# Order of the score products in an attention kernel: long blocks of all four heads ahead of the short ones

## The chip, the cores and the metric

The kernel runs on one core of a Trainium2 chip. The metric is the device time of one execution in microseconds; the median of several executions is given. The core has five engines that run side by side, each taking its own instructions in order and waiting on semaphores for the others: TensorE (PE, matrix products into PSUM), ScalarE (ACT), VectorE (DVE), GpSimd (POOL) and SyncE (SP, which issues transfers). A matmul has a stationary operand, whose load is an instruction of its own (PEld in the profile), and a moving operand whose columns stream past it. The array can be addressed in row groups of 32 partitions, so products with a 32-long contraction can stand side by side in it.

## What is computed

For 32 images of 256 channels and 1024 positions: a group normalisation, a masked self-attention with 8 heads of 32 channels, and a residual addition. All in float32.

```python
q  = einsum('oc,bcs->bos', q_w, xf) + q_b          # xf: normalised x, (32, 256, 1024)
kv = einsum('oc,bcs->bos', kv_w, xf) + kv_b
mask = tril(ones((S, S)), -1)                      # a query sees only earlier positions
scores = einsum('bhqd,bhkd->bhqk', q, k) / sqrt(dk)
scores = where(mask == 0, -10000.0, scores)
attn = softmax(scores, axis=-1)
attn = where(mask == 0, 0.0, attn)
out = einsum('bhqk,bhkd->bhqd', attn, v)
return x + out
```

## The kernel before

**Tiling.** The scores are kept transposed, keys on the partitions and queries in the columns. A group `g` is four heads (four times 32 channels fill the 128 partitions of a `q` and a `k` tile), so head `j` of a group lies in the partitions 32j to 32j+31, which is row group `j` of the array. The 1024 queries are two halves (`hf`) of 512. For one key block of 128 (`k`) and one half, `piece` says which queries are needed, since a key block is seen only by later queries. For most key blocks that is one stretch of 512 or 256 queries. Where the key block is the second one on the diagonal of its half (`d == 1`), 384 queries remain, and the free 128 columns are filled with the last key block of that half (`k + 2`), which needs 128 queries. Such a piece has two entries in `blocks`; the others have one.

**Visits.** The work on an image is a fixed list of 12 visits, 6 for each group. A visit takes one `full` piece (512 columns for each of four heads) and one `half` piece (256 columns for each):

```python
visits += [
    (f[0][0], f[0][2]), (f[0][1], h[1, 0]), (f[1][0], h[1, 1]),
    (f[1][3], h[2, 0]), (f[1][4], h[2, 1]), (f[1][5], f[1][6]),
]
```

`f[0][1]` and `f[1][5]` are the pieces with two blocks, so 4 of the 12 visits of an image have them: 128 of the 384 visits in all.

**Scores of a visit.** `scores` takes three PSUM tiles `sT` of two banks each. `pairs[0]` holds the full piece of heads 0 and 1, `pairs[1]` that of heads 2 and 3 (one bank per head), and `pairs[2]`, called `short`, holds the half piece of all four, two heads in a bank. TensorE is given: the half piece of heads 2 and 3; the full piece of heads 0, 1, 2, 3; then, behind a wait on the semaphore `bank_free` [...], the half piece of heads 0 and 1. Each float32 matmul of the program is two matmul instructions in the trace, called the first and the second pass here, each with its own weight load. A visit with one block in its full piece is therefore 16 matmul instructions, one with two blocks 24.

**What follows.** ScalarE takes the exponential of the three tiles (L331 twice, L329 once), GpSimd zeroes the masked queries on the diagonal (L292), VectorE adds the exponentials up for the softmax's sum (L358), and one visit later TensorE multiplies them with `v` into `acc` (`values`, L353). Between scores and values of a step, TensorE runs one unit of the projections of the next image (`project_qk` and `project_v`, both through `product`, L169). The main loop (L612 on) writes this order out by hand for all engines but SyncE; no scheduler moves an instruction.

**Lines of the prediction.** L272 to L282 is `scores_of`, whose loop over `blocks` sets the order within a head; L309 to L311 and L321 are its calls; L277 is the matmul itself.

Of the kernel before, what the change touches and what calls it, by code (L numbers as in the profile page):

```python
# [17 lines left out]
P = 128  # L18
HD = 32
CPG = 8  # L20
HALF = 512
# [10 lines left out]
def tile_norm_attention_residual(  # L32
# [19 lines left out]
    nc = tc.nc  # L52
# [56 lines left out]
    def unshifted():  # L109
        live = {}  # L110
# [158 lines left out]
                blocks = [(k, slice(0, HALF), slice(0, HALF))]  # L269
            return g, hf, k, part, tuple(blocks)  # L270

        def scores_of(pc, pair, j):  # L272

            b, (g, hf, k, part, blocks) = pc
            rows = slice(HD * j, HD * (j + 1))
            for kb, cols, of in blocks:
                ins = nc.tensor.matmul(  # L277
                    pair[:, cols], lhsT=live["k", b, g][rows, kb * P : (kb + 1) * P],
                    rhs=live["q", b, g][rows, hf * HALF + of.start : hf * HALF + of.stop],
                    start=True, stop=True, skip_group_check=True,  # L280
                )
            return ins  # L282

        def mask(pc, e):


            g, hf, k, part, blocks = pc
            if k < hf * BPH:
                return
            n = len(blocks)  # L290
            diagonal = e[:, :, : n * P].rearrange("p j (n q) -> p j n q", q=P)
            nc.gpsimd.affine_select(  # L292
                out=diagonal, in_=diagonal, pattern=[[0, 4], [0, n], [1, P]],
                compare_op=ALU.is_gt, fill=0.0, base=0, channel_multiplier=-1,
            )
            if k == 0:
                nc.gpsimd.memset(e[0:1, :, 0:1], 1.0)

        def scores(b, full, half, between=()):

            tag = "e0" if full[2] == 0 else "e"
            name = f"{b}_{full[0]}_{full[1]}_{full[2]}"
            e = epool.tile([P, 4, HALF], F32, tag=tag, bufs=4 if tag == "e0" else 3, name=f"{tag}_{name}")
            eh = epool.tile([P, 4, HALFBANK], F32, tag="eh", bufs=4, name=f"eh_{name}")
            pairs = [ps_s.tile([P, 2, HALF], F32, tag="sT", name=f"sT_{name}_{a}") for a in range(3)]
            short = pairs[2].rearrange("p bank (n q) -> p bank n q", n=2)
            first = [scores_of((b, half), short[:, j % 2, 1, :], j) for j in (2, 3)]  # L309
            for j in range(4):  # L310
                scores_of((b, full), pairs[j // 2][:, j % 2, :], j)  # L311

            for ins in first:
                ins.then_inc(bank_free, 1)
                tc.no_tile_sem_insts.add(ins.ins.name)
            live["free"] = live.get("free", 0) + len(first)
            wait = nc.tensor.wait_ge(bank_free, live["free"])
            for ins in first:
                tc.declare_no_dep(wait.ins, ins.ins, reason="the semaphore orders them")
            for j in range(2):  # L320
                lo = scores_of((b, half), short[:, j, 0, :], j)  # L321
                for ins in first:
                    tc.declare_no_dep(lo.ins, ins.ins, reason="the semaphore orders them")
            for a in (0, 2, 1) if between else (0, 1, 2):
                if a == 1:
                    for f in between:
                        f()
                if a == 2:
                    exp = nc.scalar.activation(eh.rearrange("p (n bank) q -> p bank n q", n=2), short, AF.Exp)  # L329
                else:  # L330
                    nc.scalar.activation(e[:, 2 * a : 2 * a + 2, :], pairs[a], AF.Exp)  # L331

            for ins in first:
                tc.add_to_no_dep_group(f"first_{name}", ins.ins)
                tc.add_to_no_dep_group("first", ins.ins)
            tc.declare_no_dep(exp.ins, group=f"first_{name}", reason="through the last two products")
            tc.declare_fence(exp.ins, group=f"first_{name}")
            mask(full, e)
            mask(half, eh)
            live["e", b, full], live["e", b, half] = e, eh  # L340
# [210 lines left out]
        with tc.manual_schedule(engines={ENG.PE, ENG.Activation, ENG.DVE, ENG.Pool}):  # L551
# [60 lines left out]
            for i in range(B * N + 1):  # L612
                if i < B * N:

                    between = at.pop(i, ()) if i % N == 6 else ()
                    scores(i // N, *visits[i % N], between)
                for f in at.pop(i, ()):
                    f()
                if i:
                    for pc in products[(i - 1) % N]:  # L620
                        values((i - 1) // N, pc, i < B * N - 1)
                for f in after.pop(i, ()):
                    f()
# [159 lines left out]
```

## Time and profile before

| | |
|---|---|
| Median of 3 executions | 1878.86 us (1873.87 to 1880.27) |
| Span of the profiled execution | 1874.0 us |
| TensorE busy | 1850.8 us, 99% |
| VectorE busy | 1573.4 us, 84% |
| ScalarE busy | 1413.7 us, 75% |
| GpSimd busy | 765.5 us, 41% |
| Score matmuls (L277) | 7168 instructions |
| Mean granted TensorE clock | 0.997 |

A row of busy time is the union of the engine's instructions, and matmuls of different row groups overlap, so 99% says that TensorE nearly always had something in flight, not that its array was full. The profile models the end of a matmul; its start is recorded. A matmul's duration in the tables runs from its recorded start, so it contains the time for which it stood behind its own weight load. The start of the next block of work is the reading to trust for how long a block took.

### The profile page before, as it was taken

To read this page: it belongs to the slowest core of one execution; us is meant where nothing else is said; L and a number is where in the kernel's file an instruction comes from. 1 tells how busy PE (TensorE), PEld (TensorE's weight loads), DVE (VectorE), ACT (ScalarE), POOL (GpSimd) and SP (SyncE) were. 2 spreads that over 40 slices of the span, in tenths; PEclk is the share of its full clock that TensorE was granted. 3 is DMA by queue.
4 is the path that set the end of the run, shared out by engine and by line. 5 is a ranking of instruction groups with operands and counts; after the bars stand their busy time and mean duration, and the time that the engine had idled before them with its cause. 6 is when DMAs were issued, how large, how long until landed. Compare 5 with 4: busy or idle time off the path is not lost.

```text
span 1874.0 us, 54145 instructions
## 1 busy us (share of the span) xinstructions
PE 1850.8 (99%) x23410; PEld 950.6 (51%) x23410; DVE 1573.4 (84%) x1604; ACT 1413.7 (75%) x1775; POOL 765.5 (41%) x741
## 2 busy tenths in 40 slices
PE   8999999999999999999999999999999999999997
PEld 4555555555554555555555545455555555455543
DVE  3778988888988889888889888898888888888878
ACT  5777777777777777777777777777777777777775
POOL 1443443434434434434344344343343443443413
PEclk9999999999999999999999999999999999999998
DMA  3446665666666666665666656766556666666412
GB/s 119 69 79 144 138 145 118 117 137 138 140 123 127 125 140 139 145 121 111 137 138 142 145 105 123 140 138 148 117 114 140 138 143 116 133 123 140 95 50 81
DMA packets 77516, 233.41 MB, mean 125 GB/s; under 512 B 19808, under 2 KB 20832, under 8 KB 61912
## 3 DMA queue, kind: packets, MB, share of 16 engines
q0 software_dynamic: 15360, 94.39, 34.4%
q1 hardware_dynamic: 60280, 134.72, 24.7%
q8 instruction: 185, 3.03, 0.7%
q10 hardware_dynamic: 1632, 0.79, 0.1%
q14 instruction: 59, 0.48, 0.1%
HBM read 68.41 MB, written 35.62 MB: 56 GB/s over the span
## 4 chain that ended last, share of the span: by engine, by line
PE 97%; DVE 1%; DMA 0%; ACT 0%; issue 0%; ACTq 0%; DVEq 0%
PE sT L277 31%; PE acc L353 26%; PE pp L169 25%; PE ppv L169 13%; PE pd L390 2%; DVE e L358 1%; DMA wn<-in_L_conv_kv_w_dram 0%; DVE rb L464 0%; DVE rb L463 0%; DVE rb L478 0%; ACT e L331 0%; PE pv L169 0%; PE busy L155 0%; ACT k L231 0%; PE pm L169 0%
## 5 line engine op out<-in xcount | busy, mean ns | idle before, releaser
L331 ACT ACTIVATE e<-sT 128x1024 f32<-128x1024 f32 x768 | 748.3, 1022 | 365.4 <-PE sT L277 283.2
L358 DVE TENSOR_TENSOR e<-e,eh 128x1024 f32<-128x1024 f32 x382 | 534.5, 1413 | 247.2 <-PE acc L353 215.1
L292 POOL TENSOR_SCALAR_AFFINE_SELECT e<-e 128x512 f32<-128x512 f32 (+1 forms) x256 | 359.4, 1404 | 678.5 <-ACT e L331 657.9
L358 DVE TENSOR_TENSOR e<-e,e 128x1536 f32<-128x1536 f32 x381 | 618.0, 1622 | 16.9 <-POOL e L292 2.6
L277 PE MATMUL sT<-q,k 32*128 32x256 f32 (+3 forms) x7168 | 617.6, 460 | 0.8 <-ACT k L231 0.8
L277 PEld LDWEIGHTS sT<-q,k 32*128 32x128 f32 x7168 | 463.4, 184 | 163.7 <-ACT q L231 50.6
L169 PE MATMUL pp<-xn,wT 128*32 128x512 f32 x4096 | 492.2, 598 | 0.0
L353 PE MATMUL acc<-e,v 128*32 128x512 f32 (+2 forms) x4096 | 401.1, 486 | 0.0
L329 ACT ACTIVATE eh<-sT 128x1024 f32<-128x1024 f32 x384 | 395.6, 1030 | 0.0
L371 POOL DMA_DIRECT2D e<-e x240 | 199.5, 892 | 388.0 <-PE sT L277 159.5
L169 PE MATMUL ppv<-wT,xn 128*32 128x256 f32 x4096 | 247.3, 382 | 0.0
L353 PEld LDWEIGHTS acc<-e,v 128*32 128x32 f32 x4096 | 132.9, 110 | 223.6 <-issue 201.1
L353 PE MATMUL acc<-eh,v 128*32 128x256 f32 x3072 | 224.4, 379 | 0.0
L169 PEld LDWEIGHTS pp<-xn,wT 128*32 128x32 f32 x4096 | 107.0, 109 | 218.2 <-issue 199.3
L353 PEld LDWEIGHTS acc<-eh,v 128*32 128x32 f32 x3072 | 98.5, 110 | 164.2 <-issue 152.6
L169 PEld LDWEIGHTS ppv<-wT,xn 128*32 128x32 f32 x4096 | 120.2, 109 | 102.0 <-issue 32.1
L292 POOL TENSOR_SCALAR_AFFINE_SELECT eh<-eh 128x512 f32<-128x512 f32 x128 | 160.6, 1255 | 0.1
L464 DVE SCALAR_TENSOR_TENSOR rb<-rb,v_bias_col,x 128x512 f32<-128x512 f32 (+1 forms) x127 | 114.1, 898 | 4.5
L463 DVE TENSOR_TENSOR rb<-num,rb 128x512 f32<-128x512 f32 (+1 forms) x127 | 90.4, 711 | 11.6 <-DMA rb<-inverses 11.3
L231 ACT ACTIVATE k<-pp,qk_bias 128x512 f32<-128x512 f32 x128 | 89.4, 698 | 13.5 <-PE pp L169 12.4
L214 DVE TENSOR_SCALAR xn<-x,mean,rstd 128x512 f32<-128x512 f32 x128 | 96.7, 796 | 2.0 <-POOL rstd L207 2.0
L231 ACT ACTIVATE q<-pp,qk_bias 128x512 f32<-128x512 f32 x128 | 89.9, 702 | 4.0 <-PE pp L169 4.0
(69 smaller groups left out, 515.2 us busy)
## 6 DMA issues: line engine op xcount, KB each, us to landing
e<-e POOLq DMA_DIRECT2D x120, 512.0 KB, 8.0
x<-in_x_dram SPq DMA_DIRECT2D x64, 512.0 KB
out_dram<-rb SPq DMA_DIRECT2D x127, 256.0 KB
rb<-inverses SPq DMA_DIRECT2D x126, 256.0 KB
e<-e POOLq DMA_DIRECT2D x120, 256.0 KB, 5.0
folded<-e SPq DMA_DIRECT2D x120, 256.0 KB
rows<-sums SPq DMA_DIRECT2D x31, 32.0 KB
inverses<-inv SPq DMA_DIRECT2D x31, 32.0 KB
```

Source lines behind the costliest of these rows:

```text
L169: nc.tensor.matmul(out[part], lhsT=lhsT[:, part], rhs=rhs, start=start, stop=stop, skip_group_check=True)
L214: nc.vector.tensor_scalar(live["xn", b][:, g, cols], live["x", b][:, g, cols], mean[:, g : g + 1], rstd[:, g : g + 1], ALU.subtract, ALU.mult,
L231: nc.scalar.activation(live[key][:, cols], pp, AF.Identity, bias=qk_bias[:, n, g : g + 1], scale=(SCALE, 1.0)[n],)
L277: ins = nc.tensor.matmul(pair[:, cols], lhsT=live["k", b, g][rows, kb * P : (kb + 1) * P], rhs=live["q", b, g][rows, hf * HALF + of.start ...
L292: nc.gpsimd.affine_select(out=diagonal, in_=diagonal, pattern=[[0, 4], [0, n], [1, P]], compare_op=ALU.is_gt, fill=0.0, base=0, channel_mu ...
L329: exp = nc.scalar.activation(eh.rearrange("p (n bank) q -> p bank n q", n=2), short, AF.Exp)
L331: nc.scalar.activation(e[:, 2 * a : 2 * a + 2, :], pairs[a], AF.Exp)
L353: nc.tensor.matmul(acc[HD * j : HD * (j + 1), of], lhsT=live["v", b][:, kb, h * HD : (h + 1) * HD], rhs=e[:, j, cols], start=first, stop=l ...
L358: nc.vector.tensor_add(total[:, :, of], total[:, :, of], e[:, :, cols])
L371: nc.gpsimd.dma_start(out=total[:rows], in_=total[rows : 2 * rows], accum_op=ALU.add)
L463: nc.vector.tensor_mul(rb, num[:, within], rb)
L464: nc.vector.scalar_tensor_tensor(rb, rb, v_bias_col[:, g : g + 1], xt[:, g, cols], ALU.add, ALU.add)
```

## The change

In a visit whose full piece has two blocks, the order on TensorE was head by head: 384 queries of head 0, 128 of head 0, 384 of head 1, 128 of head 1, and so on. After the change it is block by block: 384 queries of heads 0 to 3, then 128 queries of heads 0 to 3. The half piece stays where it was, two heads ahead and two behind. Its purpose is that neighbouring instructions belong to different row groups, as they do already in the visits with one block. Nothing is added or removed: the same 24 matmuls of such a visit run with the same operands into the same PSUM columns, and the other 256 visits have the order that they had. The order of ScalarE, VectorE, GpSimd and SyncE is the same.

```diff
-        def scores_of(pc, pair, j):
+        def scores_of(pc, pair, j, n=0):
 
             b, (g, hf, k, part, blocks) = pc
             rows = slice(HD * j, HD * (j + 1))
-            for kb, cols, of in blocks:
-                ins = nc.tensor.matmul(
-                    pair[:, cols], lhsT=live["k", b, g][rows, kb * P : (kb + 1) * P],
-                    rhs=live["q", b, g][rows, hf * HALF + of.start : hf * HALF + of.stop],
-                    start=True, stop=True, skip_group_check=True,
-                )
-            return ins
+            kb, cols, of = blocks[n]
+            return nc.tensor.matmul(
+                pair[:, cols], lhsT=live["k", b, g][rows, kb * P : (kb + 1) * P],
+                rhs=live["q", b, g][rows, hf * HALF + of.start : hf * HALF + of.stop],
+                start=True, stop=True, skip_group_check=True,
+            )
...
             first = [scores_of((b, half), short[:, j % 2, 1, :], j) for j in (2, 3)]
-            for j in range(4):
-                scores_of((b, full), pairs[j // 2][:, j % 2, :], j)
+
+
+            for n in range(len(full[4])):
+                for j in range(4):
+                    scores_of((b, full), pairs[j // 2][:, j % 2, :], j, n)
```

## The prediction

> **What bounds the kernel now.** I read the page's first part, then TensorE's own waits, then the middle of the run in one window (100 to 1700 us: PE busy 1598.24 of 1600.00 us), then two visits in the timeline, then the score matmuls kept apart by shape.
>
> ```profile
> span 1874.0 us, 54145 instructions
> PE 1850.8 (99%) x23410; PEld 950.6 (51%) x23410; DVE 1573.4 (84%) x1604; ACT 1413.7 (75%) x1775; POOL 765.5 (41%) x741
> ```
>
> TensorE is the bound. Its waits (engine, line, what it waited for: us in total, times, longest) confirm that nobody holds it up:
>
> ```profile
> PE wt L148 <- DMA wn<-in_L_conv_q_w_dram: 5.1, 1, 5.1
> PE pd L390 <- DVE e L358: 2.1, 1, 2.1
> ...
> PE sT L277 <- ACT k L231: 0.8, 1, 0.8
> ```
>
> The scores waited once, for 0.8 us, in the whole run. So what a visit costs is decided inside TensorE, and time taken out of it comes off the end unless it turns into a wait. Now a visit with one block, a visit with two, and what follows each (start us, length us, ...):
>
> ```profile
> 899.98 1.57 PE L277 MATMUL sT<-q,k 32*128 32x256 f32 x16
> 901.48 1.93 PE L169 MATMUL ppv<-wT,xn 128*32 128x256 f32 x32
> ...
> 904.73 1.67 PE L277 MATMUL sT<-q,k 32*128 32x256 f32 x24
> 906.33 1.92 PE L169 MATMUL pp<-xn,wT 128*32 128x512 f32 x16
> ```
>
> Read start to next start: 901.48 - 899.98 = 1.50 us with 16 matmuls, 906.33 - 904.73 = 1.60 us with 24. Both stream the same 768 columns through each row group. Going through the trace's starts of all 384 visits, the one-block visits take 1.502 to 1.503 us, and the two-block visits 1.600 us but for the last two (2.23 us). The difference, 0.098 us in each of 128 visits, is all that an order can win: **12.5 us**.
>
> Where do the 0.098 us sit? The shapes tell (count | busy us, mean ns of one | idle):
>
> ```profile
> L277 PE MATMUL sT<-q,k 32*128 32x256 f32 x3072 | 499.4, 400 | 0.8 <-ACT k L231 0.8
> L277 PE MATMUL sT<-q,k 32*128 32x512 f32 x2048 | 395.6, 613 | 0.0
> L277 PE MATMUL sT<-q,k 32*128 32x384 f32 x1024 | 184.6, 520 | 0.0
> L277 PE MATMUL sT<-q,k 32*128 32x128 f32 x1024 | 112.6, 269 | 0.0
> ```
>
> In the two visits of the timeline, a matmul whose weights were loaded ahead is recorded with 374 ns (256 columns), 481 (384) and 587 (512); one that starts together with its load has 478, 585 and 692, so 104 to 105 ns more. The means count the late loads. For 512: (2 x 692 + 6 x 587) / 8 = 613, two of eight per visit, the unavoidable first ones of heads 0 and 1. For 384: 520 = (3 x 585 + 5 x 481) / 8: **three** of eight. One load per two-block visit is late, always.
>
> [...] in the visit at 904.73 head 1's 384-query matmul starts at 904.752, while head 0's 128-query one, ahead of it in the program, starts at 905.488. [...]
>
> **The change, step by step.** Starts in the visit at 904.73 (us past 904), first and second pass each:
> - head 3: half piece .732, 1.052; 384 queries 1.268, 1.694; 128 queries 2.016, 2.125; then 107 ns of streaming to 2.232, and the next product starts at 2.325.
> - head 2: .725, 1.045; 1.261, 1.584; 1.906, 2.015.
> - head 1: 384 queries .752, 1.179; 128 queries 1.501, 1.610; half piece 1.722, 1.940; end 1.940 + .213 = 2.153.
>
> Between the passes of the 384 block lie 323 ns in head 2 but 426 in head 3. Head 3's load for it is recorded at 1.265, just after head 2's block began (1.261); head 2's own load was at 1.047. In the one-block visit the same two loads lie 7 ns apart (900.299, 900.306). The reason I read from the program order: [...] 17 loads and matmuls ahead of head 3's load have not started, since the 128-query blocks of heads 0, 1 and 2 stand in between; in the one-block visit it is 5. Head 1's half-piece load still came in time (1.613) with 11 unstarted ahead. [...]
>
> After the change 5 stand ahead of head 3's load, and at most about 10 ahead of any other (the half-piece load of head 1), so none is late. Then:
> - head 3: 1.268 + .323 = 1.591, + .322 = 1.913, + .109 = 2.022, end 2.129. It gains 103 ns and is no longer last.
> - head 1 becomes last. Its first issue moves up by some 7 ns (heads follow each other by 7 ns in the one-block visit, 13 here), so its end is 2.146.
> - plus the same 92 ns to the next product: 2.238 in place of 2.325.
>
> Saving 0.087 us x 128 visits = **11.1 us**; 1878.86 - 11.1 = **1867.8 us**. Of the 103 ns in head 3, 16 are lost because head 1's chain takes over. Rearranging the remaining 23 matmuls costs nothing: same shapes, same weights, each in its own row group.
>
> **What could hand it back.** The wait for `pairs[1]` to be empty now stands ahead of the 128-query blocks of heads 0 and 1. It is over long before:
>
> ```profile
> 905.99 1.94 ACT L331 ACTIVATE e<-sT 128x1024 f32<-128x1024 f32 x2 [0.86 <-DVE e L358]
> 907.81 1.03 ACT L329 ACTIVATE eh<-sT 128x1024 f32<-128x1024 f32 x1
> ```
>
> The last exponential of this visit ends at 908.84, the next scores start at 909.47: 0.63 us of slack, of which the change eats 0.09. The first exponential waits for head 1's second 128-query pass (1.610 before, 1.603 after), so it keeps its place in the visit. If completions were signalled in program order it would wait for head 3's 384 block too, some 0.2 us later, still inside the slack. VectorE, at 84%, would have 1573.4 / 1863 = 84.5%. [...]
>
> **Rivals.**
> 1. The whole difference goes: two-block visits become as short as the others, 12.5 us, 1866.4 us. For: the columns are equal. Against: head 1's chain has two more passes to start, and measures 1.188 us from first to last start against 1.178 in the one-block visit.
> 2. No gain: the late load is not a matter of place in the queue [...], or the saving comes back as waits. 1878.9 us. Against: 128-query passes average 269 ns, with their own loads in time; the slack is 0.63 us.
> 3. Slower: the late load moves to a head that has no reserve. One late load in head 1 puts its end at 2.253, the next product at 2.345, 0.020 us later than now: +2.6 us, 1881.5 us. Two in a row would give 0.127 us: +16 us, 1895 us. For: block-by-block order packs heads 0 and 1 tighter. Against: their loads have fewer unstarted instructions ahead than before.
>
> **Chances.** My forecast 0.72, rival 1 0.10, rival 2 0.13, rival 3 0.05. The executions before spread from 1873.87 to 1880.27, so I take 3 us either way around forecast and rival 1 and let the range reach partway to rival 2: 1862.5 to 1874. Faster by over 0.3% (5.6 us) 0.82, within 0.13, slower 0.05.
>
> **What would show it.** Right: two-block visits of 1.51 us start to next start; mean of the 384-query matmuls 507 ns (2 x 585 + 6 x 481, by 8) in place of 520, those of 512, 256 and 128 unchanged; head 3's first 384 load some 7 ns after head 2's; no new TensorE wait over 1 us. Wrong: two-block visits still at 1.60 us, or shorter visits with the span unchanged and a TensorE wait on ACT or POOL in their place.

## The result and the profile after

The time did not move. The changed kernel takes 1879.74 us (median of 6, 1877.66 to 1886.01) against 1879.57 us for the kernel before (median of 6); the ratio is 1.0011, 95% interval 0.9988 to 1.0035. Measured again with 22 executions, the ratio is 0.9992 (0.9984 to 1.0001). The forecast was 1867.8 us, with a range up to 1874.

Inside the visits everything came as worked out. The first fence is the page of the profiled execution after the change, the second the timeline of a two-block visit, of what follows it and of its first exponential on ScalarE (start us, length us), the third the score matmuls kept apart by shape between 100 and 480 us, where no stall lies.

```profile
span 1883.9 us, 54145 instructions
PE 1845.2 (98%) x23410; PEld 932.3 (49%) x23410; DVE 1572.1 (83%) x1604; ACT 1413.1 (75%) x1775; POOL 768.3 (41%) x741
```

```profile
905.03 1.58 PE L277 MATMUL sT<-q,k 32*128 32x256 f32 x24
906.55 1.93 PE L169 MATMUL pp<-xn,wT 128*32 128x512 f32 x16
...
906.51 1.94 ACT L333 ACTIVATE e<-sT 128x1024 f32<-128x1024 f32 x2 [1.07 <-PE sT L277]
```

```profile
L277 PE MATMUL sT<-q,k 32*128 32x512 f32 x424 | 81.9, 613 | 0.0
...
L277 PE MATMUL sT<-q,k 32*128 32x384 f32 x216 | 36.0, 507 | 0.0
```

A two-block visit now takes 906.55 - 905.03 = 1.52 us as printed, and 1.512 to 1.513 us in the records of nearly all of them; the mean of the 384-query matmuls is 507 ns, so the third late load is gone (over the whole run the mean is 516 ns, because the matmuls of stalled visits are recorded longer). TensorE is busy for 1845.2 us, 5.6 us less. Yet this execution's span is 9.9 us longer than the one profiled before. Part of that is the choice of execution: this one is the slowest of the six, the one before was among the faster ones. A second profile of the changed kernel, with a time near its median, has a span of 1875.5 us; the 11.1 us are missing there too. So TensorE stands idle somewhere. Its waits (engine, line, what it waited for: us in total, times, longest), and its idle time before the `pd` products of all images but the last two:

```profile
PE pd L392 <- ACT num L363: 4.6, 3, 1.8
PE pd L392 <- issue: 4.2, 2, 2.2
...
PE pd L392 <- DMA folded<-e: 3.7, 2, 2.1
PE pv L169 <- DVE dev L196: 1.9, 5, 0.7
```

```profile
L392 PE MATMUL pd<-folded,pick_half 128*32 128x512 f32 x240 | 32.9, 619 | 13.8 <-ACT num L363 4.6 <-issue 4.2 <-DMA folded<-e 3.7
```

`pd` are the products that sum the folded exponentials of an image over the key rows (`sum_folded`); they read what SyncE's transfer `folded` brings. The view names ScalarE or "issue" for most of these waits, but in the nine long ones ScalarE's last signal stands 0.2 to 1.4 us ahead of `pd`; where the landing of `folded` is recorded (twice) it comes last, 0.1 to 0.2 us ahead. The kernel before waited there for about 2 us in its profiled execution. The trace shows the pattern image by image. I take the time from the first score of an image to the first score of the next, for the 29 images in the steady part:

| kernel | shortest, us | sum of what is over the shortest, us | images over by more than 0.3 us |
|---|---|---|---|
| before | 57.20 | 2.3 | 2 |
| after, first profile | 56.84 | 23.1 | 9 |
| after, second profile | 56.84 | 11.9 | 9 |

An undisturbed image is 0.35 us shorter, 4 visits x 0.088 us, and 32 x 0.35 = 11.2 us: the gain is there. Nine images in 29 give it back, up to 4.7 us each.

The 23.1 us of the first profile have three parts, read from where a stalled image falls behind an undisturbed one. 15.5 us are lost at `pd`. 2.4 us are lost at `pv`, a small product of the next normalisation for which TensorE waits for VectorE directly. 4.9 us are lost just behind `pd` in three images: at 1206.0, 1380.1 and 1612.2 us, after the three longest waits at `pd` (2.0 to 2.2 us), the granted clock is recorded at 0.50 for 3.41 us (half of that is 1.7 us). After the waits of 1.8 us or less it stayed at 1.00. The second profile has no wait as long and no such stretch in its steady part.

What holds such an image up is a chain through several engines. VectorE finishes an earlier image (two before the one whose scores run) with the reciprocals of its sums, which come by DMA (`rb<-inverses`). Its stores follow, and behind them SyncE issues the load of a later image's `x`, into the buffer that the finished image leaves. The fences have VectorE's waits for the reciprocals, first in the kernel before, then in the kernel after:

```profile
DVE rb L463 <- DMA rb<-inverses: 11.3, 11, 2.5
```

```profile
DVE rb L465 <- DMA rb<-inverses: 39.6, 30, 2.9
```

Then SyncE. Here is its timeline for one stalled image, with TensorE's `pd` behind it, and then for the image after it, which was not stalled. A row that covers several issues (x2) runs from the first to the end of the last.

```profile
786.41 1.44 SPq L117 DMA_DIRECT2D x<-in_x_dram  x2
788.67 14.37 SPq L379 DMA_DIRECT2D folded<-e  x2
```

```profile
800.51 1.07 PE L392 MATMUL pd<-folded,pick_half 128*32 128x512 f32 x8 [1.59 <-DMA folded<-e]
```

```profile
841.64 1.91 SPq L117 DMA_DIRECT2D x<-in_x_dram  x2
848.73 11.09 SPq L379 DMA_DIRECT2D folded<-e  x2
```

```profile
857.38 1.04 PE L392 MATMUL pd<-folded,pick_half 128*32 128x512 f32 x8
```

Count from the first score of each image's window (765.77 and 824.79 us in the trace). In the stalled image VectorE waits 1.76 and 0.73 us for reciprocals (and 1.75 us more ahead of its last product with them, put down to a store), the last store is issued at 20.3 us in place of 16.5, the load of `x` at 20.6 in place of 16.9, and the folded sums of the last group at 22.9, only 2.3 us behind it. They land just ahead of 800.5, about 11.8 us after their issue. In the other image they are issued 7.1 us behind the load of `x`, and `pd` starts 8.65 us later without a wait. The folded sums of the stalled image are not issued later than those of the other (22.9 us against 23.9), they only take longer.

The other images fit. In the 18 stalled ones of the two profiles the load of `x` is issued at 19.35 us or later, and `pd` starts 12.8 to 15.3 us behind it; in the others it is issued by 18.1 us, but for one at 19.34. No experiment moved the load of `x` alone, so this link is read from the traces and not tested.

### The profile page after: what moved, and what is told of

Its sections match the earlier page's. It is cut to its first block, busy times and chain, and to the rows that moved or that the text cites. A ratio compares the mean times of both kernels' runs of the same rounds, so it can differ in the third digit from the quotient of the medians.

```text
span 1883.9 us, 54145 instructions
## 1 busy us (share of the span) xinstructions
PE 1845.2 (98%) x23410; PEld 932.3 (49%) x23410; DVE 1572.1 (83%) x1604; ACT 1413.1 (75%) x1775; POOL 768.3 (41%) x741
## 5 line engine op out<-in xcount | busy, mean ns | idle before, releaser
L277 PE MATMUL sT<-q,k 32*128 32x256 f32 (+3 forms) x7168 | 610.0, 460 | 0.8 <-ACT k L231 0.8
L277 PEld LDWEIGHTS sT<-q,k 32*128 32x128 f32 x7168 | 446.6, 185 | 172.2 <-ACT eh L331 65.2
L465 DVE TENSOR_TENSOR rb<-num,rb 128x512 f32<-128x512 f32 (+1 forms) x127 | 89.9, 708 | 42.2 <-DMA rb<-inverses 39.6
L466 DVE SCALAR_TENSOR_TENSOR rb<-rb,v_bias_col,x 128x512 f32<-128x512 f32 (+1 forms) x127 | 109.6, 863 | 4.5
L214 DVE TENSOR_SCALAR xn<-x,mean,rstd 128x512 f32<-128x512 f32 x128 | 91.4, 755 | 1.6 <-POOL rstd L207 1.6
```

Source lines behind the costliest of these rows:

```text
L214: nc.vector.tensor_scalar(live["xn", b][:, g, cols], live["x", b][:, g, cols], mean[:, g : g + 1], rstd[:, g : g + 1], ALU.subtract, ALU.mult,
L277: return nc.tensor.matmul(pair[:, cols], lhsT=live["k", b, g][rows, kb * P : (kb + 1) * P], rhs=live["q", b, g][rows, hf * HALF + of.start ...
L465: nc.vector.tensor_mul(rb, num[:, within], rb)
L466: nc.vector.scalar_tensor_tensor(rb, rb, v_bias_col[:, g : g + 1], xt[:, g, cols], ALU.add, ALU.add)
```

## The experiments

Theory A: the shorter visits take margin from this loop (reciprocals by DMA, VectorE's finish, stores, load of x, folded sums, `pd`), whose transfers take as long as before (the folding transfers land 8.0 and 4.8 us after their issue by the median, 8.0 and 5.0 in the kernel before). Theory B: it is the exponentials themselves. In the trace the first exponential of a two-block visit starts 1.21 to 1.26 us into it before and 1.43 to 1.48 us after, though the matmul that it needs starts at the same place (0.885 and 0.878 us). Theory C: the gain is lost in some third way.

**Reciprocals one visit earlier, in both kernels.** The same edit in the changed kernel and in the kernel before:

```diff
-                    when(v + 2, lambda b=b: check_sums(b, every))
-                    when(v + 2, lambda b=b: invert(b, every))
+                    when(v + (2 if late else 1), lambda b=b: check_sums(b, every))
+                    when(v + (2 if late else 1), lambda b=b: invert(b, every))
```

> The changed kernel with one more edit: the sums' range test and reciprocal on VectorE, and with them the transfers of the reciprocals, come one visit (4.7 us) earlier. Theory A (the 11 us were handed back by the transfer loop: reciprocals land late, so VectorE finishes the image late, so the stores, the load of the next x and behind it the folded sums are late, and TensorE waits for these at the pd products): the loop gets 4.7 us of margin, TensorE's waits at pd fall from 16 us to under 2 us, and the time is 1862 to 1866 us, 0.993 of the kernel before. Theory B (the later signal to the first exponential, 0.21 us in each two-block visit, is what costs): the waits stay, 1874 us or more. Theory C (the shorter visits do not reach the end for another reason): 1874 us or more with no waits at pd.

> The kernel before, old order of the scores, with the same one-visit-earlier reciprocals. Theory A: the kernel before had some of these waits too, 2 us in its profile and more in its slower executions, so this goes to its floor of about 1873.5 us and its executions spread less than 3 us. The gap to the changed kernel with the same edit is 11 us. Theories B and C: no change from the kernel before (1876 to 1880 us).

Measured: changed kernel 1864.35 us, ratio 0.9931 (0.9918 to 0.9943); kernel before 1875.02 us, 0.9981 (0.9974 to 0.9989). The gap is 10.7 us. The page and VectorE's longest waits in the changed kernel with the edit:

```profile
span 1860.4 us, 54088 instructions
```

```profile
DVE e L360 <- ACT eh L331: 100.6, 46, 5.4
DVE e L360 <- PE acc L355: 90.3, 40, 15.0
DVE e L360 <- POOL e L291: 24.6, 25, 1.0
```

No row for `rb` is left in that view at all, and the images sum to 0.4 us over the shortest. This is what theory A asked for: with margin in the loop, the change is worth what its visits are worth. The kernel before gains 3.3 us from the same edit, so it had been paying too; its executions spread by 4.4 us and not by the less than 3 us that was expected.

**`pd` one visit later.** One line in the changed kernel:

```diff
-                        when(first + N + 6, lambda b=b: sum_folded(b), after)
+                        when(first + N + 7, lambda b=b: sum_folded(b), after)
```

> The changed kernel with TensorE's products on the folded sums (pd) one visit later, the reciprocals where they were. Theory A: the wait of TensorE is cut at its last link, since the folded sums then have 4.7 us more to land, though VectorE still waits for late reciprocals; 1862 to 1868 us. If the lateness of VectorE reaches TensorE by another way too (through values or the next projections), more, 1870 us. Theory B: no change, 1876 us or more.

Measured: 1880.37 us, ratio 1.001 (1.0003 to 1.0017), outside what theory A expected. The stalls did go (0.6 us over the shortest, no image over by 0.3 us), but the shortest image grew from 56.85 to 57.35 us. Two things make it: `pd` now meets its PSUM bank while ScalarE is still emptying it, in every image, and at its old place it had filled the time in which the following scores would have waited for an exponential (that visit takes 1.56 us here, not 1.513).

```profile
PE pd L392 <- ACT q L231: 7.9, 31, 0.5
...
DVE rb L465 <- DMA rb<-inverses: 5.1, 4, 2.5
```

So 0.5 us x 30 images = 15 us of new, steady cost cancels what the stalls cost. The second line shows that the run did not cut the last link alone: VectorE's waits for reciprocals fell as well, from 39.6 to 5.1 us. The period is longer, and the reciprocals have their margin back. So the run is in keeping with theory A, but it tests neither the last link nor its worth.

**Order by pairs of heads.** Long and short blocks of heads 0 and 1, then of heads 2 and 3:

```diff
-            for n in range(len(full[4])):
-                for j in range(4):
-                    scores_of((b, full), pairs[j // 2][:, j % 2, :], j, n)
+            for a in range(2):
+                for n in range(len(full[4])):
+                    for j in (2 * a, 2 * a + 1):
+                        scores_of((b, full), pairs[a][:, j % 2, :], j, n)
```

> The long and short blocks ordered by pairs of heads: 384 queries of heads 0 and 1, 128 of heads 0 and 1, then the same for heads 2 and 3. Head 3's first load then has 13 unstarted instructions ahead, between the 11 that were in time and the 17 that were not. If 13 is in time, two-block visits take 1.51 us as in the changed kernel, and the first exponential starts 1.21 to 1.26 us into them, as before, not 1.43 to 1.48. Theory B: then 1866 to 1869 us. Theory A: the visits are as short as in the changed kernel, so most of the gain is handed back all the same, 1873 to 1880 us. If 13 is too many, 1.60 us a visit and 1876 to 1880 us.

Measured: 1870.5 us, ratio 0.9958 (0.9943 to 0.9973), between the two expectations. Two-block visits take 1.513 us (so no load was late here, with 13 unstarted instructions ahead of head 3's), and the first exponential starts 1.20 to 1.25 us into them. One visit, what follows it and its first exponential:

```profile
908.48 1.58 PE L277 MATMUL sT<-q,k 32*128 32x256 f32 x24
909.99 1.92 PE L169 MATMUL pp<-xn,wT 128*32 128x512 f32 x16
...
909.72 1.94 ACT L334 ACTIVATE e<-sT 128x1024 f32<-128x1024 f32 x2 [0.52 <-PE sT L277]
```

The images sum to 5.2 us over the shortest. With TensorE's visits equally short, the earlier start of the exponentials is worth 7 to 9 us, more than half of what the changed kernel loses.

**The exponentials late, and nothing else.** The kernel before, ScalarE taking heads 2 and 3 first in two-block visits:

```diff
-            for a in (0, 2, 1) if between else (0, 1, 2):
+            for a in (0, 2, 1) if between else (1, 0, 2) if len(full[4]) > 1 else (0, 1, 2):
```

> The kernel before, but in the 128 two-block visits ScalarE takes the exponential of heads 2 and 3 ahead of that of heads 0 and 1, so its first one starts some 0.4 us later into the visit, while TensorE's order and its 1.60 us stay. Theory A: later exponentials make the sums and the folding transfers later against the reciprocal, the reciprocals land later, waits on VectorE for them rise from 11 us to 30 us or more, and the time to 1881 to 1890 us. Theory C (the exponentials have slack and their start does not matter): as the kernel before, 1876 to 1880 us.

Measured: 1896.48 us, ratio 1.0077 (1.0048 to 1.0106), the way that theory A expected and by more than its range. VectorE's wait for reciprocals:

```profile
DVE rb L463 <- DMA rb<-inverses: 56.0, 40, 2.3
```

A two-block visit and its first exponential in that kernel, in TensorE's and in ScalarE's timeline:

```profile
914.23 1.67 PE L277 MATMUL sT<-q,k 32*128 32x256 f32 x24
915.83 1.92 PE L169 MATMUL pp<-xn,wT 128*32 128x512 f32 x16
```

```profile
915.98 1.94 ACT L331 ACTIVATE e<-sT 128x1024 f32<-128x1024 f32 x2 [1.35 <-POOL rstd L207]
```

TensorE's visit is still 1.60 us, the exponential starts 1.75 us into it, and the images sum to 22.7 us over the same shortest 57.20. Here 6.0 us of TensorE's waits, 7 in number, are at `pv`, for VectorE directly; the load of `x` and `pd` are not the only way in which a late VectorE reaches TensorE. Half a microsecond on ScalarE, in visits where ScalarE idles anyway, costs more than the change could bring.

**Both together with early reciprocals.** Does lateness of the exponentials cost in any other way? Two kernels: the order by pairs with early reciprocals, and the swapped exponentials with early reciprocals.

> Order by pairs of heads, and the reciprocals one visit earlier. Theory A, as it now stands (all of what the order by pairs lost against 11 us came from the collision of the reciprocals' transfers with the folding transfers): both kernels with early reciprocals sit on the same floor, so this is 1862 to 1866 us, ratio 0.992 to 0.994, although its first exponentials are 0.22 us earlier than in the changed kernel with early reciprocals. Theory B (later exponentials cost TensorE time directly): faster than that kernel by 3 us or more, 1857 to 1861 us.

> The kernel before with the exponentials swapped in the two-block visits (first one some 0.5 us later) and the reciprocals one visit earlier. Theory A (later exponentials cost only through the late reciprocals): the 14 us that the swap cost go away, 1873 to 1877 us, ratio 0.997 to 0.999, as the kernel before with early reciprocals; no waits for reciprocals on VectorE. Theory B (later exponentials hold TensorE up directly as well): 1880 us or more.

Measured: 1864.57 us, 0.9926 (0.9913 to 0.9938), and 1875.3 us, 0.9983 (0.9975 to 0.9991). The first compares with 1864.35 us for the changed kernel with early reciprocals, whose exponentials are later, the second with 1875.02 us for the kernel before with early reciprocals, whose exponentials are earlier: 0.2 and 0.3 us apart. Theory B as a cost of its own falls: in these kernels late exponentials cost nothing once the reciprocals have margin.

**Which transfers are in the way.** In the trace, GpSimd issues two folding transfers (512 and 256 KB) ahead of the reciprocal. The median time from the last of them to the reciprocal, and from the reciprocal to the issue of the first read-back of what it wrote to memory (a negative time means that the reciprocal came first):

| kernel | last fold to reciprocal, us | reciprocal to first read-back, us | VectorE's waits for reciprocals, us |
|---|---|---|---|
| before | 5.17 | 4.12 | 11.3 |
| order by pairs | 5.03 | 4.42 | 9.5 |
| after, first and second profile | 4.82, 4.71 | 4.96, 4.65 | 39.6, 39.6 |
| before, exponentials swapped | 4.60 | 4.78 | 56.0 |
| after, early reciprocals | -1.24 | 2.07 | 0 |

The later the exponentials, the closer the folds stand ahead of the reciprocals' write; that they hold the write up is a reading of this table. To test it, the folds of the third group go one visit later, behind the write:

```diff
                     else:
+                        v += n == 2
                         when(v, lambda b=b, n=n: fold(b, n, 2 * HD), after)
```

> The changed kernel, reciprocals where they were, but the folding transfers of the third of the four score groups (and its stacking) one visit later, so that they are issued behind the reciprocals' write and not 5 us ahead of it. Theory A (the write of the reciprocals stands behind these transfers): the time from the reciprocal to the first read-back drops from 5.0 us to 2 to 3 us as in the kernel with early reciprocals, the waits for reciprocals on VectorE go from 40 us to under 10 us, 1862 to 1868 us. Theory D (what helped there was only that everything came 4.7 us earlier, not the order against the folding transfers): no gain, 1876 us or more.

Measured: 1878.63 us, ratio 1.0002 (0.9988 to 1.0016), which is what theory D expected and not theory A. The step came as expected and its effect did not:

```profile
DVE rb L465 <- DMA rb<-inverses: 43.6, 30, 3.3
```

The first read-back starts 2.73 us after the reciprocal, as expected, but the fold is now issued in the middle of the four read-backs, and VectorE waits for them as long as ever. That the write alone is held up is thereby ruled out. Two readings are left: the folds cost the reciprocals time wherever on their way the two meet, or the early reciprocals helped by their 4.7 us of margin alone (theory D). No run tells these apart, nor whether the transfers share queues or DMA engines.

**The changed kernel again.**

> The changed kernel as it is, a second time beside the others: 1877 to 1886 us, ratio 0.999 to 1.004; waits of TensorE at pd of 5 us or more and VectorE's waits for reciprocals of 25 us or more in its profile.

Measured: 1877.26 us (median of 22), ratio 0.9992 (0.9984 to 1.0001); 8.8 us of TensorE's idle time before `pd`, 39.6 us of waits for reciprocals. Its executions run from 1872.78 to 1880.89 us, those of the kernel before, measured beside it (35 executions), from 1873.87 to 1884.59, the 6 with early reciprocals only from 1862.50 to 1865.31.

## Why the prediction was wrong, point by point

- **TensorE bounds the kernel: right, but only to the floor.** The profiled execution before, at 1876.05 us with 2.3 us of stalls, was near the good end of a kernel that ranges from 1872 to 1885 us. I read "nobody holds it up" from it. With early reciprocals the same TensorE work takes 1875.0 us and spreads by less than 5 us.
- **The late load and its worth: right.** 384-query mean 507 ns where nothing stalls, visits of 1.512 us, 0.088 us saved against 0.087 forecast, head 1's chain last (modelled end 1.582 us into the visit, head 3's 1.566). Where nothing else interferes, the change is worth 10.7 us against 11.1 forecast.
- **The reason of the late load: only in part.** That the order decides it is shown: head by head one load is late (visits of 1.600 us), in both other orders none (1.512 to 1.513 us). That the number of unstarted instructions decides it was my estimate, and "so none is late" with it; the runs do not show it. The 17 are counted at 0.329 us into the visit, 2 ns after head 3's second half-piece pass started; head 2's load for the same block had started 2 ns after head 2's pass. At 0.455 us the number ahead of head 3's load had fallen to 13, and the load started only at 0.540 us; in the order by pairs 13 stand ahead of it, and the visits are as short as in the changed kernel. What decides it was not shown.
- **"What could hand it back": the step that failed.** I counted the slack of TensorE's own waits (0.63 us) and a mean occupancy of VectorE, and looked for a wait of TensorE on the exponentials alone; the transfers behind VectorE were put at nothing. I took it that the first exponential "keeps its place in the visit". I named the 0.2 us by which it would slip if completions came in program order, called it "still inside the slack", and stopped. It did slip, by 0.21 us, and this was the larger part of the loss: the order by pairs, with visits of the same length and the exponentials in their old place, brings 0.9958 in place of 0.9992 to 1.0011. The rest comes with the shorter period, which the order by pairs has too: early reciprocals bring it 5.9 us, where they brought the kernel before 3.3.
- **Program order: read from the starts only.** The two starts that the prediction sets side by side are out of program order. The signal that the first exponential waits for is not. It is raised by head 1's last 128-query matmul; the trace records it at 1.190 us into the visit before, at 1.403 after, at 1.173 in the order by pairs, though that matmul starts at 0.885, 0.878 and 0.879. After the change it comes 0.06 us behind the modelled end (1.346 us) of head 3's second 384-query pass, which stands ahead of it in the program.
- **Figures of the steps.** The 107 and 213 ns of streaming are what the recorded lengths show: 267, 374, 481 and 587 ns for 128, 256, 384 and 512 columns, ends modelled. The 107 ns of a late load in rival 3 are an estimate; in the trace a late load cost 104 to 105 ns.
- **The view that would have told it was at hand.** VectorE's waits of the kernel before list 11 waits for `rb<-inverses`, 11.3 us. A wait that shows up in a third of the images is one without margin, and what stands behind it ends at TensorE.
- **Rival 2** named the right outcome (1878.9 us) with "the saving comes back as waits", at a chance of 0.13. What it had against itself, the slack of 0.63 us, was the slack of the wrong wait. The wait was not on ScalarE or GpSimd at the scores, as the prediction's signs had it, but mostly on a transfer at `pd`.
- **Rivals 1 and 3** did not occur: head 1's two extra passes cost the 10 ns that separate 1.512 from 1.502, and no other load became late.

## What to carry to other kernels

When one engine is at 99%, a gain on it shortens the period of everything else; look in the other engines' waits for transfers that already arrive late in some of the rounds, because here those took no less time than before (4.12 us from the reciprocal to its first read-back before, 4.96 and 4.65 after) and had just lost margin. A wait of an engine with idle time is not harmless if its instructions are in order and something of a later round stands behind it. Executions that spread about as much as the change is worth can be a sign of such a loop, as they were here, and giving it room (here a reciprocal one visit earlier) is then the first edit to try: it brought 3.3 us by itself, and 14 us together with the change.

## What the runs showed of the hardware

- TensorE started matmuls of different row groups out of program order (904.752 us for head 1's 384-query matmul, 905.488 for head 0's 128-query matmul, ahead of it in the program). The signal that the first exponential waits for did not come out of order. In the changed kernel head 1's last pass for the first exponential starts at 0.878 us into the visit, when head 3's second 384 pass (0.865 us), ahead of it in the program, has just started; the signal comes at 1.403 us and the exponential starts at 1.43 to 1.48 us. In the order by pairs, where no block of heads 2 and 3 but their half pieces precedes it in the program, the signal comes at 1.173 us and the exponential starts at 1.20 to 1.25 us.
- Not every weight load came ahead: in the head-by-head order head 3's load for its 384-query block started 213 ns after head 3's second half-piece pass, head 2's 2 ns after its own. The matmul that starts with the late load is recorded with 584 ns in place of 481, and the visits take 1.600 us, 126 of the 128 alike; in the other two orders they take 1.512 to 1.513 us.
- A long wait of TensorE cost more than itself. In the first profile after the change, each of the three waits of 2.0 to 2.2 us at `pd` was followed by a stretch of 3.41 us at a granted clock of 0.50, which lost another 1.6 to 1.7 us each; after its waits of 1.8 us or less the clock is recorded at 1.00.
- TensorE's undisturbed visits repeat to 1 ns over the whole run; the executions spread through the stalls and, by up to 3.3 us, through the start (the first score starts 17.7 to 20.9 us into the eleven profiled executions). With early reciprocals the spread of the changed kernel fell from 8 us (22 executions) to 3 us (6), that of the kernel before from 11 us (35) to 4 us (22).
